# Two levels of Strassen for the weight products of layer 0 in a two-layer graph network kernel, with block sums lent to VectorE

## The chip, the cores and the metric

The kernel runs on one core of one Trainium2 chip. The metric is the device time in microseconds (us) of one execution. All runs told here that were timed in rounds were in the fast state. A profile is one execution taken by the hardware profiler; its span is about 2 us shorter than the time of the same run, and a little different from run to run.

## The reference

128 graphs of 128 nodes, 512 features, all fp32. Cut to what matters:

```python
# layer 0
deg = jnp.sum(adj, axis=-1, keepdims=True)
agg = jnp.einsum('bij,bjf->bif', adj, x) / jnp.maximum(deg, EPS)
out = jax.nn.relu(jnp.einsum('bnf,of->bno', concat([x, agg]), W))
x   = _layernorm(x + out)
# layer 1: three times adj @ (x @ W) + b, with relu after the first two
x   = _layernorm(x + gcn3(gcn2(gcn1(x))))
```

The kernel rewrites layer 0 as `x @ WA + adj_normalized @ (x @ WB)`. These two, `x @ WB` (called y) and `x @ WA`, are the "weight products of layer 0". The graphs go in 32 groups of four; a group's layer 1 is interleaved with the next group's layer 0.

## The kernel before

Everything is planned ahead by a list scheduler in the kernel's own Python. Each operation names its engine, an estimated length, what it reads and writes, and whether it uses the SBUF port that VectorE and GpSimd share. The planner keeps a clock per engine and one for the shared port, and returns an order, in which the operations are then emitted. It counts as users of the port every GpSimd operation and VectorE's sums with both inputs in SBUF; VectorE's sums that read PSUM, and its small layernorm instructions, it lets pass.

```python
class Plan:
    AHEAD = 24
    ...
    def start(o, t):
        ...
        if o.shared:
            port = (o.engine, end)
    ...
            for e in engines[1:]:
                ...
                can = [
                    o for o in known[e]
                    if ready_at[o] <= t and has_room(o, t) and not (o.shared and port[0] != e and port[1] > t)
                ]
                ...
                o = min(can, key=lambda o: (o.latest, o.n))
                ...
                start(o, t)
```

The emission is two lines. Note what they do not contain: the port is a clock in the planner and nothing else.

```python
    for o in plan.order():
        o.emit()
    return plan
```

A 512x512 weight product is one level of Strassen-Winograd: 7 block products of 4 matmuls with 256 columns. Sums of data blocks go to GpSimd, sums of weights to VectorE, PSUM partial results through ScalarE copies and VectorE sums.

```python
    class Data:
        def sums(self):
            for d, a, b, op in ((4, 2, 3, OP.add), (5, 4, 0, OP.subtract), ...):
                add("POOL", F, const(self.t[:, d]), const(self.t[:, a]), const(self.t[:, b]), ...)
    ...
    def product(p, a, b, k, start, transposed):
        ...
            for o in range(2):
                for c in range(2):
                    ...
                    nc.tensor.matmul(bank_ap(p)[:, o, :], lhsT, rhs, ...)   # 256 columns
    ...
    def wino_a(key, a, b, c00, c11, transposed=False, inner=None):
        product(py, a, b, 1, True, transposed)
        s1 = copied(py)                       # ScalarE, PSUM to SBUF
        product(pz, a, b, 5, True, transposed)
        ...
```

The last product of a group, which matters below, multiplies the adjacency by a 512-wide row block `row` that VectorE has to take out of PSUM first:

```python
    def seg_last(q, m):
        s, u = row(q, "s3"), u_of(q)
        ...
            nc.tensor.matmul(bank_ap(p)..., a[:, g, :], s.t[:, g, :], start=True, stop=True, ...)
        # then + u, layernorm, store
```

## Time and profile before

The median was 2423.59 us in the three runs known ahead of the prediction, and 2424.42 us (2420.16 to 2426.06, four runs) with one more.

| | before |
|---|---|
| span of the profile | 2426.3 us |
| TensorE busy | 2390.6 us, 99% |
| VectorE, ScalarE, GpSimd busy | 36%, 33%, 37% |
| TensorE work, matmuls times their spacing | 2382 us |
| one group in the steady part | 74.47 us |

The page's lines and how they are read stand in the prediction. In one sentence: TensorE runs at its own spacing from 80 us to the end, but for some 10 us, so its work is nearly the whole time, and the other engines have two thirds of theirs free.

### The profile page before, as it was taken

To read this page: it belongs to the slowest core of one execution; us is meant where nothing else is said; L and a number is where in the kernel's file an instruction comes from. 1 tells how busy PE (TensorE), PEld (TensorE's weight loads), DVE (VectorE), ACT (ScalarE), POOL (GpSimd) and SP (SyncE) were. 2 spreads that over 40 slices of the span, in tenths; PEclk is the share of its full clock that TensorE was granted. 3 is DMA by queue.
4 is the path that set the end of the run, shared out by engine and by line. 5 is a ranking of instruction groups with operands and counts; after the bars stand their busy time and mean duration, and the time that the engine had idled before them with its cause. 6 is when DMAs were issued, how large, how long until landed. Compare 5 with 4: busy or idle time off the path is not lost.

```text
span 2426.3 us, 29271 instructions
## 1 busy us (share of the span) xinstructions
PE 2390.6 (99%) x11776; PEld 2079.8 (86%) x11776; DVE 864.1 (36%) x1685; ACT 800.6 (33%) x1345; POOL 895.2 (37%) x772
## 2 busy tenths in 40 slices
PE   7999999999999999999999999999999999999997
PEld 6888888888888888888888888888888888888886
DVE  5433332333333333332343333333323433233323
ACT  2233333233332333233333333333233333333333
POOL 3333433334333344332443333433334432344323
PEclk9999999999999999999999999999999999999999
DMA  8201211112111121110111111211111111011100
GB/s 208 57 30 63 66 49 57 44 48 65 53 56 48 40 65 57 53 61 27 65 57 53 61 41 51 66 57 53 51 37 61 53 48 61 22 61 55 42 18 35
DMA packets 56360, 133.30 MB, mean 55 GB/s; under 512 B 21920, under 2 KB 27040, under 8 KB 48160
## 3 DMA queue, kind: packets, MB, share of 16 engines
q1 hardware_dynamic: 55552, 131.16, 16.9%
q8 instruction: 93, 1.52, 0.3%
q14 instruction: 43, 0.35, 0.1%
q10 hardware_dynamic: 672, 0.26, 0.1%
HBM read 97.78 MB, written 33.62 MB: 54 GB/s over the span
## 4 chain that ended last, share of the span: by engine, by line
PE 95%; DMA 3%; DVE 1%; issue 0%; ACT 0%; SPq 0%; POOL 0%; ACTq 0%; POOLq 0%; DVEq 0%
PE bank L408 77%; PE bank L646 5%; PE bank L687 5%; PE bank L421 4%; PE bank L563 4%; DMA dd<-deg 2%; DMA r<-dd 1%; DMA xT<-in_xT_dram 0%; DVE st L489 0%; SPq L265 0%; DVE deg L374 0%; DVE ah L275 0%; DVE row L275 0%; DVE deg L375 0%; ACT s L394 0%
## 5 line engine op out<-in xcount | busy, mean ns | idle before, releaser
L273 POOL TENSOR_TENSOR T<-T 128x512 f32<-128x512 f32 x384 | 484.9, 1274 | 1225.0 <-ACT T L656 970.1
L408 PE MATMUL bank<-w,T 128*128 128x256 f32 x3584 | 800.1, 379 | 2.3 <-ACT s L394 2.3
L408 PEld LDWEIGHTS bank<-w,T 128*128 128x128 f32 x3584 | 675.9, 190 | 92.8 <-ACT s L394 2.3
L394 ACT COPY s<-bank 128x512 f32<-128x512 f32 x480 | 281.3, 586 | 1225.5 <-PE bank L408 1225.2
L275 DVE TENSOR_TENSOR row<-bank,s 128x512 f32<-128x512 f32 x288 | 198.8, 691 | 690.5 <-PE bank L408 545.3
L408 PE MATMUL bank<-wb,xT 128*128 128x256 f32 x1792 | 404.5, 380 | 6.0 <-DMA wb<-in_w0T_dram 5.6
L408 PEld LDWEIGHTS bank<-T,w 128*128 128x128 f32 x1792 | 340.3, 190 | 74.5 <-issue 31.3
L408 PE MATMUL bank<-T,w 128*128 128x256 f32 x1792 | 397.8, 379 | 1.5 <-issue 1.5
L408 PE MATMUL bank<-wa,xT 128*128 128x256 f32 x1792 | 397.7, 379 | 0.0
L408 PEld LDWEIGHTS bank<-wb,xT 128*128 128x128 f32 x1792 | 341.5, 191 | 53.3 <-issue 5.6
L408 PEld LDWEIGHTS bank<-wa,xT 128*128 128x128 f32 x1792 | 340.5, 190 | 46.3
L273 POOL TENSOR_TENSOR u<-u,b 128x512 f32<-128x512 f32 x128 | 164.3, 1285 | 188.0 <-PE bank L563 186.4
L273 POOL TENSOR_TENSOR xT<-xT 128x512 f32<-128x512 f32 x128 | 163.8, 1280 | 61.6 <-DMA xT<-in_xT_dram 49.4
L563 PEld LDWEIGHTS bank<-at,u 128*128 128x128 f32 x1024 | 130.9, 195 | 12.4 <-ACT u L506 6.8
L563 PE MATMUL bank<-at,u 128*128 128x128 f32 x1024 | 132.3, 279 | 6.4 <-ACT u L506 6.4
L275 DVE TENSOR_TENSOR bank<-bank,s 128x512 f32<-128x512 f32 x96 | 67.2, 700 | 195.3 <-PE bank L421 195.3
L421 PE MATMUL bank<-row,ah 128*128 128x256 f32 x512 | 126.2, 379 | 2.3 <-DVE ah L275 2.3
L687 PE MATMUL bank<-row,at 128*128 128x512 f32 x256 | 120.5, 594 | 5.6 <-DVE row L275 5.6
L646 PEld LDWEIGHTS bank<-at,row 128*128 128x128 f32 x1024 | 119.4, 192 | 1.7
L530 DVE SCALAR_TENSOR_TENSOR u<-bank,x 128x512 f32<-128x512 f32 x128 | 88.3, 690 | 89.7 <-PE bank L421 87.5
L590 ACT ACTIVATE T<-T,b 128x256 f32<-128x256 f32 x192 | 90.5, 503 | 89.0 <-DVE T L275 89.0
L646 PE MATMUL bank<-at,row 128*128 128x128 f32 x1024 | 119.5, 275 | 0.0
(30 smaller groups left out, 1226.1 us busy)
## 6 DMA issues: line engine op xcount, KB each, us to landing
x<-in_x_dram SPq DMA_DIRECT2D x32, 1024.0 KB, 6.5
out_dram<-o SPq DMA_DIRECT2D x64, 512.0 KB, 2.6
xT<-in_xT_dram SPq DMA_DIRECT2D x31, 1024.0 KB, 4.8
ar<-in_adj_dram SPq DMA_DIRECT2D x32, 256.0 KB, 2.8
at<-in_adjT_dram SPq DMA_DIRECT2D x32, 256.0 KB, 2.6
r<-dd SPq DMA_DIRECT2D x31, 256.0 KB, 4.5
w<-in_w_dram SPq DMA_DIRECT2D x12, 256.0 KB, 10.1
xT<-in_xT_dram SPq DMA_DIRECT2D x4, 256.0 KB, 5.0
```

The lines of the kernel that those rows point to most:

```text
L273: gpsimd(n, lambda: pinned(nc.gpsimd.tensor_tensor(dst(), a(), b(), op=op)), reads, writes)
L275: vector(n, lambda: pinned(nc.vector.tensor_tensor(dst(), a(), b(), op=op)), reads, writes, shared)
L394: scalar(512, lambda: pinned(nc.scalar.copy(S_T[s.index], bank_ap(p))), [p], [s])
L408: nc.tensor.matmul(bank_ap(p)[:, o, :], lhsT, rhs, start=start and o == 0 and c == 0, stop=c == 1, skip_group_check=True,)
L421: nc.tensor.matmul(bank_ap(p)[:, j, :], AH_T[:, g, :], y.t[:, g, h * H : (h + 1) * H], start=False, stop=True, skip_group_check=True,)
L530: nc.vector.scalar_tensor_tensor(u.ap(m, h), bank_ap(p), 0.0, X.ap(m, h), op0=OP.max, op1=OP.add)
L563: nc.tensor.matmul(bank_ap(p)[:, c // 2, (c % 2) * P : (c % 2 + 1) * P], u.t[:, g, c * P : (c + 1) * P], a[:, g, :], start=True, stop=True ...
L590: lambda t=t, o=o: pinned(nc.scalar.activation(t, t, AF.Relu, bias=B1_T[:, 2 * h + o : 2 * h + o + 1])),
L646: nc.tensor.matmul(bank_ap(p)[:, g // 2, (g % 2) * P : (g % 2 + 1) * P], s.t[:, g, o * P : (o + 1) * P], a[:, g, :], start=True, stop=True ...
L687: nc.tensor.matmul(bank_ap(p).rearrange("p a n -> p (a n)"), a[:, g, :], s.t[:, g, :], start=True, stop=True, skip_group_check=True,)
```

## The change

It replaces the outer 7 products of layer 0's two weight products by 7 x 7 inner ones: 49 matmuls of 128 columns for 28 matmuls of 256 columns, which in 128-column units is 49 for 56. For this it needs block sums of block sums. Per group there are eight more sums of x, six sums that combine the inner results (and two that finish), and many PSUM evacuations with 384 elements. GpSimd alone could not take all these in time, so the planner may give a GpSimd block sum to VectorE when it is urgent (`HELP`). To fit, the diff also reorders the blocks of x, y and u, keeps fewer buffers for the adjacency, loads and sums the next group's adjacency later in the group, and stores each graph's output apart; no run separates these.

The diff, cut to its core (cuts marked `...`):

```diff
+    AHEAD, HELP = 24, 4.0
...
+                if e == "DVE":
+                    can += [
+                        o for o in known["POOL"]
+                        if o.other and ready_at[o] <= t and o.latest + slip < t + self.HELP and has_room(o, t)
+                        and not (port[0] != e and port[1] > t)
+                    ]
...
+                known[o.engine].remove(o)
+                if o.engine != e:
+                    o.engine, (o.us, o.emit) = e, o.other
...
+        def inner_sums(self):                      # class Data
+            for ps in BATCH:                       # 4 of the 7 outer blocks, then 3
+                t, ti = self.t[:, ps[0] : ps[-1] + 1], self.ti[:, :, ps[0] : ps[-1] + 1]
+                a00, a10, a01, a11 = (t[:, :, c, g] for c in range(2) for g in range(2))
...
+                    add("POOL", len(ps) * P, const(dst), const(a), const(b), reads, writes, op)
...
+    def inner_product(p, a, b, ps, i, start):
+        parts = [(a.inner(k, i), b.inner(k, i)) for k in ps]
+        def emit():
+            for n, ((ta, _), (tb, _)) in enumerate(parts):
+                    nc.tensor.matmul(quarters(p, 4)[:, n], ta, tb, ...)     # 128 columns
...
     def seg_y_a(q):
         y = row(q, "y")
-        wino_a(("y", q), XA, WB, sums_to(y, 0, 0), sums_to(y, 1, 1))
+        def c11(u3, p5, keys):
+            add("POOL", F, const(y.ap(1, 1)), u3, p5, keys, y.block(1, 1))
+        outer_a(("y", q), XA, WB, c11)
...
     XA.sums()
     WB.sums()
+    XA.inner_sums()
+    WB.inner_sums()
```

`XI_T` (written `xI` in the profile) holds the new inner sums of x; `xT` the blocks of x and their outer sums; `T` the blocks of layer 1's data; `v` the half-combined inner results.

## The prediction

> **What bounds the kernel now.** I read the page's first two parts, then the chain that ended last, then the instruction groups by shape, then a table of stretches and the timeline of the start.
>
> ```profile
> span 2426.3 us, 29271 instructions
> PE 2390.6 (99%) x11776; PEld 2079.8 (86%) x11776; DVE 864.1 (36%) x1685; ACT 800.6 (33%) x1345; POOL 895.2 (37%) x772
> PE 95%; DMA 3%; DVE 1%; issue 0%; ACT 0%; SPq 0%; POOL 0%; ACTq 0%; POOLq 0%; DVEq 0%
> ```
>
> TensorE is busy 99% and makes up 95% of the chain; the other three engines are idle for two thirds of the span. "Busy" is not yet "at its rate", so the spacing of matmuls has to come from the chain. One group of four graphs in the steady part:
>
> ```profile
> 1112.71 34.53 PE bank L408 x160
> 1148.11 3.57 PE bank L646 x32
> 1157.73 10.36 PE bank L408 x48
> 1173.33 1.78 PE bank L563 x16
> 1175.11 1.72 PE bank L687 x4
> ```
>
> Columns: start, length, what. There are two matmul records for each fp32 matmul of the program (11776 records for 5888). A 256-column record takes 34.53/160 = 0.2158 us, a 128-column one 1.78/16 = 0.1113 us (3.57/32 = 0.1116 in the other place), a 512-column one 1.72/4 = 0.43 us. The group rows' means (379 and 279 ns) are pipelined durations and not spacings: 160 records of 379 ns would not fit into 34.53 us.
>
> ```profile
> 0.00:51.48 51.48, 36.82 (x161) 31.80 (x161) 29.75 (x52) 9.87 (x15) 11.22 (x12) 0.90 0.90 229
> 437.76:1112.71 674.95, 670.73 (x3314) 584.09 (x3313) 236.13 (x469) 224.76 (x379) 250.62 (x216) 1.00 0.17 53
> 1112.71:2304.18 1191.47, 1191.47 (x5890) 1038.10 (x5889) 416.64 (x818) 399.97 (x673) 445.48 (x384) 1.00 0.16 52
> ```
>
> Columns: stretch, length, busy time of PE, PEld, DVE, ACT, POOL, then clock, DMA share, GB/s. In the last stretch, sixteen groups (74.47 us each), TensorE never stops. Counting the built program: 1024 matmuls of 128 columns, 4736 of 256, 128 of 512. At two records each: 1024 x 0.2226 + 4736 x 0.4316 + 128 x 0.86 = 228 + 2044 + 110 = 2382 us. The span is 2426, so 44 us are gaps: about 20 before the second layer's first product at 51.5 us, about 16 behind the last matmul and between the lone last group's steps, and some 8 in the middle, mostly a wait for the degrees' round trip through DRAM. The kernel is TensorE plus a start and an end.
>
> **What the Trainium skill says.** (1) "TensorE: Matmul & The Clock Gate", section "Back-to-back issue gap": a warm matmul costs N/2.4 + 2.5 ns, and in streams of weight load and matmul pairs both set the spacing. The trace fits if an fp32 record streams twice its columns: 512/2.4 + 2.5 = 215.8 ns for 256, and 109 for 128. (2) Same page, "LDWEIGHTS (loading the stationary operand)": P/1.2, so 107 ns for 128 columns whatever follows. A 128-column matmul is thus as short as a weight load can hide under; the measured 111.3 to 111.6 ns, with a fresh weight per matmul and waits every few matmuls, says that it is still hidden, at 2% over the formula. I use the measured number. (3) "SBUF — State Buffer", section "SBUF: two separate sides": VectorE with two SBUF inputs and GpSimd hold a shared port pair exclusively, and the loser waits out the whole instruction. The trace agrees: the same 512-element VectorE sum of weights takes 0.68 us alone and 1.2 us beside GpSimd:
>
> ```profile
> 7.00 4.92 DVE L275 TENSOR_TENSOR wb<-wb 128x512 f32<-128x512 f32 x4 [6.13 <-DMA wb<-in_w0T_dram]
> 8.43 5.85 POOL L273 TENSOR_TENSOR xT<-xT 128x512 f32<-128x512 f32 x4 [7.99 <-DMA xT<-in_xT_dram]
> 18.28 0.68 DVE L275 TENSOR_TENSOR wa<-wa 128x512 f32<-128x512 f32 x1
> ```
>
> (4) "GPSIMD Engine Reference", section "Engine selection": a two-input sum is about half as fast there as on VectorE. The rows agree:
>
> ```profile
> L273 POOL TENSOR_TENSOR T<-T 128x512 f32<-128x512 f32 x384 | 484.9, 1274 | 1225.0 <-ACT T L656 970.1 <-ACT T L618 232.9 <-ACT T L573 7.1
> L275 DVE TENSOR_TENSOR row<-bank,s 128x512 f32<-128x512 f32 x288 | 198.8, 691 | 690.5 <-PE bank L408 545.3 <-ACT s L394 144.0
> ```
>
> **The change, part by part.** *TensorE.* A layer-0 product was 7 block products of 4 matmuls of 256 columns, 28 x 0.4316 = 12.08 us. It becomes 49 matmuls of 128 columns, 49 x 0.2226 = 10.91 us: 1.18 us less, twice per group, so 2.35. It is not 49/56 of the time, because a half-length matmul costs 0.1113 and not 0.1079. The aggregation had 8 matmuls of 256 (3.45 us) and gets 2 of 256 and 12 of 128 (0.86 + 2.67 = 3.53): 0.08 more. Net 2.27 us per group, 32 groups: 72.7 us. The built program says the same: 4544 x 0.2226 + 2752 x 0.4316 + 110 = 2310 us, against 2382.
>
> *VectorE and GpSimd.* Per group there are now eight inner sums of x, six more sums in the outer combination, two finishing ones, and PSUM evacuations of 384 elements. Since the planner may give block sums to VectorE, the count in the built program matters: SBUF-only sums on VectorE go from 52 to 630 of 512 elements plus 103 of 384, PSUM ones gain 480 of 384; GpSimd falls from 640 to 454 (plus 33 short ones). At 0.69 us, an estimated 0.53 for 384 elements (three quarters of 0.691 and a little), and 1.28 on GpSimd: VectorE 864 + 399 + 55 + 254 = about 1570 us (67% of 2350), GpSimd 895 - 237 + 32 = 690 us (29%). ScalarE gains 32 copies of 0.59, 19 us. No engine comes near TensorE's 98%, so in the steady part these lie beside it. I also looked at each turn in which TensorE waits for another engine that itself waits for TensorE: in the order of the changed program, all but some 30 of about 1700 such waits have at least 0.75 us more TensorE work in between than one evacuation needs (0.59 us on ScalarE, 0.69 on VectorE, 0.15 for signals). In the kernel before 90 had only 0.25 to 0.5 us to spare, and they did not stall.
>
> *The start.* This is what the change adds to the path. Before, TensorE starts at 5.6 us on raw blocks. Now even the first inner product is accumulated over four blocks, three of them sums, so seven outer sums stand ahead of it on VectorE (spaced 0.60 us when alone: instructions start at 18.28, 18.88 and 19.48 us in the timeline): first matmul near 12 us. Then VectorE has a hundred instructions before the layernorm scale that releases the first graph product (before: some 40): about 52 of 512 elements at 0.60 us spacing, 32 of 384 at 0.47, a dozen small ones, 48 us, some 5 us of port collisions, and two or three of waits. From 7 us on that ends near 63, where the kernel before began its graph products at 44.9. TensorE has by then about 31 us of work in front of them (10.9 + 10.9 + 3.5 + 5.6 pulled in from the next group), so 32 us idle, against 20 before: +12 us. The three weight matrices of layer 1 and everything later wait no longer than before, and the end of the kernel is unchanged.
>
> *Sum.* 2423.6 - 72.7 + 12 = 2363. For drift between planned and real order in the steady part (port collisions, in-order VectorE) I add 3: **2366 us**, 2.4% less.
>
> **Rivals.** *VectorE becomes the bound in stretches.* It goes from 36 to 67% and is in order, with evacuations queued behind block sums and sums held out by GpSimd. For: it is the only engine whose load nearly doubles, and before there were three places where TensorE stopped because VectorE stood at a degree reduction waiting for a transfer. Against: the slack above. If each of 32 groups lost 1 us, 2395; that would be "within 2%". *The 128-column matmul does not hold its spacing* where two thirds of all records are such, each with another weight and a wait every 6 to 8. For: 107 ns of weight load in a slot of 111 ns has no room. Against: both places where the trace has such streams hold it, up to 32 in a row. 2 ns more would cost 7040 added records x 2 ns, 14 us: 2380. *The start costs nothing*, because GpSimd is free there and the degrees' transfers (11 us) already hold layer 0 up to 38 us before: then 2352. *Or it costs 25*, if the long VectorE list meets more collisions: 2378. *Transfers* become more and smaller (128 stores for 64, split loads of x); at 16% share they stay hidden.
>
> **Range and chances.** TensorE's gain is sure to about 8 us; the start may be 0 to 25 us worse; steady stalls 0 to 30, rather few. That gives 2345 to 2392. The limit for 2% is 2375.1. Faster by over 2%: 0.70; within 2%: 0.28; slower by over 2%: 0.02.
>
> **What would show it.** In the changed profile: a chain over 90% PE, with inner-product pieces at 0.111 us per record (wrong if 0.115 or more); a steady group of 72.2 us instead of 74.47; a stretch table in which PE stays at its length and VectorE at some two thirds; first graph product at 60 to 66 us; the idle of TensorE before it near 32 us. If the steady group is 73.5 us with TensorE waiting for VectorE, the first rival holds. If the VectorE sums of block data average well over 0.75 us, the port collides more than the plan allowed for.

## The result, and the profile after

The changed kernel is correct and takes 2453.41 us (median of 4 runs, 2452.49 to 2456.52); the kernel before took 2424.42 us in the same rounds. The ratio is 1.0125 (95% interval 1.0107 to 1.0142). Ratios here are the mean time of one kernel's fast runs over that of the other's of the same rounds, so not quite the ratio of the medians. So the change cost 1.2% where 2.4% were expected to be won, and the time is outside the predicted range of 2345 to 2392.

From the page of the changed kernel: span, busy time of the engines, and the chain that ended last by engine.

```profile
span 2450.7 us, 36879 instructions
PE 2344.8 (96%) x14848; PEld 2120.0 (87%) x14848; DVE 1666.5 (68%) x2878; ACT 817.3 (33%) x1377; POOL 777.8 (32%) x619
PE 82%; DVE 16%; issue 2%; DMA 0%; ACT 0%; POOL 0%; SPq 0%; ACTq 0%; DVEq 0%; POOLq 0%
```

TensorE's share of the chain has fallen from 95% to 82%, and VectorE has come in with 16%, although VectorE is busy only 68% of the span. An engine that is idle a third of the time sets the end here. The stretch table of the steady part agrees (columns as in the prediction):

```profile
1110.00:2300.00 1190.00, 1155.23 (x7353) 1045.39 (x7352) 815.82 (x1392) 404.25 (x683) 386.86 (x305) 1.00 0.16 52
```

TensorE is idle for 35 us of these 1190, where before it never stopped. What it waits for stands in one line of the waits (columns: who waited for what, us in total, how many times, longest):

```profile
PE bank L875 <- DVE row L288: 63.0, 29, 2.2
```

29 waits of 2.2 us, about one per group, all in front of the group's last product, all for VectorE's evacuation of `row`. The TensorE work itself is as planned: an inner product's pieces hold 0.111 us per record, as in this line of the timeline (start, length, what), 0.89 us from one piece of eight to the next:

```profile
1189.36 1.05 PE L518 MATMUL bank<-wb,xT 128*128 128x128 f32 x8
1190.25 1.06 PE L518 MATMUL bank<-wb,xI 128*128 128x128 f32 x8
1191.14 1.06 PE L518 MATMUL bank<-wb,xT 128*128 128x128 f32 x8
```

So why is `row` late? First the VectorE groups by shape (line, engine, operation, out<-in, shape, count, then busy time and mean length in ns of one, then idle before). Six sums into `xI` per group, and the sums of `T`:

```profile
L288 DVE TENSOR_TENSOR T<-T 128x512 f32<-128x512 f32 x216 | 201.0, 950 | 102.4 <-ACT T L810 60.2 <-ACT T L848 37.9 <-POOL T L290 2.2
L288 DVE TENSOR_TENSOR xI<-xI,xT 128x512 f32<-128x512 f32 x32 | 54.0, 1687 | 0.0
L288 DVE TENSOR_TENSOR xI<-xT 128x512 f32<-128x512 f32 x32 | 52.9, 1654 | 0.0
L288 DVE TENSOR_TENSOR xI<-xT 128x384 f32<-128x384 f32 x31 | 48.1, 1551 | 0.0
L288 DVE TENSOR_TENSOR xI<-xT,xI 128x512 f32<-128x512 f32 x32 | 21.7, 679 | 0.0
```

Three of the six sums into `xI` last 1.55 to 1.69 us in the mean of all groups, while one of the same shape takes 0.68 us. They do not sum slowly; they are held out. By whom, the timeline of one such place shows (VectorE's, GpSimd's and TensorE's rows; other rows cut):

```profile
1260.14 2.50 POOL L290 TENSOR_TENSOR xT<-xT 128x512 f32<-128x512 f32 x2 [3.90 <-PE bank L754]
...
1261.38 1.28 DVE L676 TENSOR_SCALAR rstd<-mv 128x2 f32<-128x2 f32 x1
...
1263.39 3.26 POOL L290 TENSOR_TENSOR u<-u,b 128x512 f32<-128x512 f32 x2
1263.77 3.29 DVE L288 TENSOR_TENSOR xI<-xT 128x512 f32<-128x512 f32 x2
...
1266.61 1.58 POOL L290 TENSOR_TENSOR xT<-xT 128x512 f32<-128x512 f32 x1
...
1266.99 2.22 DVE L288 TENSOR_TENSOR xI<-xI,xT 128x512 f32<-128x512 f32 x2
...
1269.13 1.15 DVE L288 TENSOR_TENSOR xI<-xT,xI 128x512 f32<-128x512 f32 x2
1270.20 0.68 DVE L288 TENSOR_TENSOR row<-bank,s 128x512 f32<-128x512 f32 x1
...
1270.94 1.98 PE L875 MATMUL bank<-row,at 128*128 128x512 f32 x4 [2.18 <-DVE row L288]
```

Read it downwards. From 1263.39 to 1268.2 GpSimd adds the bias b3 to `u` twice and makes a sum of `xT`; from 1263.77 on VectorE makes sums into `xI`. While both are at work each of VectorE's takes 1.65 us and each of GpSimd's 1.6: one waits out the other, turn by turn. As soon as GpSimd is through, two sums take 1.15 us together. `row` stands behind these six in VectorE's queue. It starts 6.43 us after the first of them, and TensorE has by then been idle for 2.18 us.

In the order that the planner returned, GpSimd's two additions and its `xT` sum come after VectorE's sums into `xI`. GpSimd ran them before. Nothing in the program tells it not to: their data are ready, it waits for no semaphore of VectorE's, and nothing else is left ahead of them in its own queue. In the built program, by my count, 204 of GpSimd's 487 sums are free to start before the VectorE block sum that stands ahead of them in the plan (a recount from the planner's dependencies alone gives some 250). The plan's turns on the port are not in the program.

To see where all the time went I took, in each trace, the distance from one TensorE record to the next, less the record's own spacing (0.1113, 0.2158 or 0.43 us by shape). Columns 1 and 2 are what the change did:

| us | before | after | GpSimd waits (below) | first group one level (below) |
|---|---|---|---|---|
| TensorE work | 2382.1 | 2309.4 | 2309.4 | 2311.7 |
| until the first matmul | 5.6 | 9.4 | 9.1 | 6.1 |
| lost from there to 80 us | 16.4 | 32.8 | 30.7 | 22.7 |
| lost from 80 us to the last matmul | 10.3 | 88.9 | 8.7 | 6.3 |
| behind the last matmul | 12 | 10 | 10 | 10 |
| span | 2426.3 | 2450.7 | 2368.1 | 2356.9 |

The 72.7 us of work are won. The start takes back 20, and the stretch behind it 79, of which 63.0 us are the 29 waits above; of the other 26 us that are lost there, some 16 are TensorE records next to these waits that come at a wider distance, and 9.5 lie elsewhere, about as much as in the kernel before.

### The profile page after: what moved, and what is told of

It is laid out like the page before. It is cut to its first block, busy times and chain, and to the rows that moved or that the text cites. A ratio compares the mean times of both kernels' runs of the same rounds, so it can differ in the third digit from the quotient of the medians.

```text
span 2450.7 us, 36879 instructions
## 1 busy us (share of the span) xinstructions
PE 2344.8 (96%) x14848; PEld 2120.0 (87%) x14848; DVE 1666.5 (68%) x2878; ACT 817.3 (33%) x1377; POOL 777.8 (32%) x619
## 4 chain that ended last, share of the span: by engine, by line
PE 82%; DVE 16%; issue 2%; DMA 0%; ACT 0%; POOL 0%; SPq 0%; ACTq 0%; DVEq 0%; POOLq 0%
PE bank L488 42%; PE bank L518 26%; DVE xI L288 7%; PE bank L838 5%; PE bank L531 4%; PE bank L875 3%; PE bank L754 3%; DVE row L288 2%; DVE xT L288 2%; DVE rstd L676 1%; PE bank L500 1%; DVE st L672 1%; DVE bank L288 1%; DVE u L727 1%; DMA xT<-in_xT_dram 0%
## 5 line engine op out<-in xcount | busy, mean ns | idle before, releaser
L488 PE MATMUL bank<-w,T 128*128 128x256 f32 x3584 | 821.3, 379 | 2.9 <-ACT s L474 2.9
L488 PEld LDWEIGHTS bank<-w,T 128*128 128x128 f32 x3584 | 659.3, 190 | 82.3 <-ACT s L474 3.2
L290 POOL TENSOR_TENSOR T<-T 128x512 f32<-128x512 f32 x168 | 213.6, 1279 | 884.3 <-DVE T L288 876.5
L488 PE MATMUL bank<-T,w 128*128 128x256 f32 x1792 | 403.7, 380 | 0.1
L488 PEld LDWEIGHTS bank<-T,w 128*128 128x128 f32 x1792 | 333.5, 190 | 52.8 <-issue 10.4
L288 DVE TENSOR_TENSOR v<-bank,s 128x512 f32<-128x512 f32 x192 | 132.2, 689 | 205.0 <-ACT s L474 113.7
L288 DVE TENSOR_TENSOR T<-T 128x512 f32<-128x512 f32 x216 | 201.0, 950 | 102.4 <-ACT T L810 60.2
L288 DVE TENSOR_TENSOR row<-bank,s 128x512 f32<-128x512 f32 (+1 forms) x288 | 179.9, 642 | 120.2 <-PE bank L488 102.1
L290 POOL TENSOR_TENSOR xT<-xT 128x512 f32<-128x512 f32 (+1 forms) x126 | 172.9, 1383 | 138.2 <-PE bank L754 112.7
L288 DVE TENSOR_TENSOR s<-bank,v 128x384 f32<-128x384 f32 x192 | 107.0, 558 | 150.6 <-PE bank L518 146.2
L288 DVE TENSOR_TENSOR v<-v 128x512 f32<-128x512 f32 x189 | 149.3, 790 | 9.9 <-DVE v L288 0.5
L518 PEld LDWEIGHTS bank<-wb,xT 128*128 128x128 f32 x896 | 115.7, 196 | 31.1 <-issue 23.2
L754 PEld LDWEIGHTS bank<-at,u 128*128 128x128 f32 x1024 | 124.7, 192 | 19.2 <-issue 15.6
L518 PE MATMUL bank<-wb,xT 128*128 128x128 f32 x896 | 124.7, 280 | 16.7 <-DMA xT<-in_xT_dram 9.4
L518 PEld LDWEIGHTS bank<-wb_i,xT 128*128 128x128 f32 x896 | 120.8, 193 | 10.6 <-DVE wb_i L288 1.4
L754 PE MATMUL bank<-at,u 128*128 128x128 f32 x1024 | 124.7, 275 | 1.3 <-ACT u L689 1.3
```

The lines of the kernel that those rows point to most:

```text
L288: on_vector = lambda: pinned(nc.vector.tensor_tensor(dst(), a(), b(), op=op))
L290: on_gpsimd = lambda: pinned(nc.gpsimd.tensor_tensor(dst(), a(), b(), op=op))
L488: nc.tensor.matmul(bank_ap(p)[:, o, :], lhsT, rhs, start=start and o == 0 and c == 0, stop=c == 1, skip_group_check=True,)
L518: nc.tensor.matmul(quarters(p, 4)[:, n], ta, tb, start=start and n == 0, stop=True, skip_group_check=True)
L754: nc.tensor.matmul(bank_ap(p)[:, c // 2, (c % 2) * P : (c % 2 + 1) * P], u.chunk(g, c), a[:, g, :], start=True, stop=True, skip_group_chec ...
```

## The experiments

Two theories are tested. **Theory A**: the plan's port turns are not enforced, GpSimd goes ahead of its turn, VectorE's in-order queue is late, and TensorE waits. **Theory B**, the rival: VectorE simply has too much to do around the last product, whoever has the port (the first rival of the prediction).

### 1. The plan's port order, enforced

The order of instructions stays as it is. Wherever an operation that uses the port follows one of the other engine in the plan, it now waits for it.

```diff
+    port = None
     for o in plan.order():
-        o.emit()
+        ins = o.emit()
+        if o.shared and ins is not None:
+            if port is not None and port[0] != o.engine:
+                tc.add_manual_dep(ins.ins, port[1].ins.name, <semaphore wait>, reason="port")
+            port = o.engine, ins
```

> The changed kernel with the same instructions in the same order on every engine, plus semaphore waits that make VectorE and GpSimd take the shared SBUF port in the order in which the planner gave it to them (in the changed kernel 204 of GpSimd's 487 sums are free to start before the VectorE block sum that stands ahead of them). Theory A (the gap of 2.2 us per group before the last product is VectorE's block sums being held out by GpSimd sums that start early): the sums of xT into xI fall from 1.55 to 1.75 us to 0.55 to 0.7, TensorE's wait for the row evacuation falls from 63 us to under 15, time 2380 (2365 to 2400). Theory B (VectorE has too many instructions ahead of the evacuation, port or not): the wait stays above 45 us, time 2440 to 2456. Theory C (the order holds, but holding GpSimd back makes its own sums late): a new wait of TensorE for GpSimd sums, time 2400 to 2440.

Measured: correct, 2376.22 us (2374.84 to 2377.03, 4 runs), the kernel before at 2430.55 (7 runs), ratio 0.9777 (0.9759 to 0.9795). Its page, and VectorE's groups by shape:

```profile
PE 2330.1 (98%) x14848; PEld 2121.5 (89%) x14848; DVE 1553.4 (65%) x2878; ACT 814.6 (34%) x1377; POOL 688.4 (29%) x619
PE 98%; DVE 1%; issue 0%; POOL 0%; ACT 0%; DMA 0%; SPq 0%; ACTq 0%; DVEq 0%; POOLq 0%
```

```profile
L288 DVE TENSOR_TENSOR T<-T 128x512 f32<-128x512 f32 x216 | 143.7, 685 | 101.9 <-ACT T L810 60.2 <-ACT T L848 37.9 <-POOL T L290 1.9
L288 DVE TENSOR_TENSOR xI<-xT 128x512 f32<-128x512 f32 x32 | 21.7, 679 | 0.0
L288 DVE TENSOR_TENSOR xI<-xI,xT 128x512 f32<-128x512 f32 x32 | 21.7, 679 | 0.0
```

TensorE's row for the last product, which in the changed kernel had 63.0 us of idle time before it:

```profile
L875 PE MATMUL bank<-row,at 128*128 128x512 f32 x256 | 120.4, 593 | 0.0
```

Not one instruction was moved, removed or made smaller; waits were only added, and the kernel became 3.4% faster than the changed kernel in ratio to the kernel before (0.9777 against 1.0125). The wait before the last product is gone. The group is now 72.28 us in the mean (26 groups from the fourth on), against 75.12 in the changed kernel and 74.71 before (counted the same way, so with the degree waits in it; a group without one took 74.47). VectorE's and GpSimd's busy times fall by 113 and 89 us: that was the time spent held out, counted as busy. Theory B falls: VectorE does the same work in the same order.

### 2. Only one of the two waits

Which of the two engines goes ahead of its turn to harm? Two kernels, each with one half of the waits.

```diff
-            if port is not None and port[0] != o.engine:
+            if port is not None and port[0] != o.engine and o.engine == "POOL":   # GpSimd waits
+            if port is not None and port[0] != o.engine and o.engine == "DVE":    # VectorE waits
```

> The changed kernel with the same order of instructions, and waits between neighbours on the shared SBUF port only where GpSimd is the one that follows (GpSimd waits for VectorE's sums that stand ahead of it; VectorE waits for nothing new). Theory A (GpSimd starts its sums some 4 us before its turn, and the in-order VectorE delivers row late): this half is the one that matters, so the time is 2370 to 2385 us, sums into xI average 0.6 to 0.75 us, and the idle time before L875 is gone. Rival (both directions matter, VectorE running into GpSimd's turn costs as much): 2400 to 2430 us.

> The other half: VectorE waits for GpSimd's sums that stand ahead of it, GpSimd waits for nothing new. Theory A: the early GpSimd sums stay, so sums into xI stay at 1.5 to 1.75 us, the gap of about 2.2 us before L875 stays, and the time is 2445 to 2465 us. Rival (any wait that separates the two cures it): 2375 to 2400 us.

Measured, on one chip, with the kernel before at 2427.89 us (7 runs): GpSimd waits, 2372.59 us (2369.88 to 2377.81, 4 runs), ratio 0.9775 (0.9753 to 0.9796). VectorE waits, 2497.4 us (2495.12 to 2498.33, 4 runs), ratio 1.0285 (1.0266 to 1.0304). Both are correct. The half that makes GpSimd wait does all that the whole does. The other half is worse than no wait at all, and by more than I expected (the range ended at 2465). The wait before the last product is what it was in the changed kernel, 63.0 us, and a second one has come: layer 1's products (L488) now wait 24.8 us for sums into `T`, where the changed kernel shows 0.1 us of idle in this row. Two rows of the page's groups, and the changed kernel's row for layer 1's products:

```profile
L488 PE MATMUL bank<-T,w 128*128 128x256 f32 x1792 | 403.9, 380 | 24.8 <-DVE T L288 23.6
...
L875 PE MATMUL bank<-row,at 128*128 128x512 f32 x256 | 135.9, 657 | 63.0 <-DVE row L288 63.0
```

```profile
L488 PE MATMUL bank<-T,w 128*128 128x256 f32 x1792 | 403.7, 380 | 0.1
```

That fits a VectorE which now also stands still for GpSimd, while GpSimd still goes ahead of its turn; which of its waits made up these 25 us I did not separate. They are not all of the loss against the changed kernel: the trace also has 14 stretches at half the granted clock between 80 and 2400 us, 47.8 us in all, where the changed kernel has 3 with 10.2, so TensorE runs slowly for a part of the time.

The same place in the kernel where GpSimd waits (its timeline, other rows cut), to be laid beside the one of the changed kernel:

```profile
1221.76 1.15 DVE L288 TENSOR_TENSOR xI<-xT 128x512 f32<-128x512 f32 x2
...
1222.17 1.88 PE L875 MATMUL bank<-row,at 128*128 128x512 f32 x4
...
1222.83 1.15 DVE L288 TENSOR_TENSOR xI<-xI,xT 128x512 f32<-128x512 f32 x2
...
1223.90 1.15 DVE L288 TENSOR_TENSOR xI<-xT,xI 128x512 f32<-128x512 f32 x2
...
1224.97 0.68 DVE L288 TENSOR_TENSOR row<-bank,s 128x512 f32<-128x512 f32 x1
...
1225.13 0.69 POOL L677 TENSOR_TENSOR rstd<-rstd,neg_half 128x2 f32<-128x2 f32 x1 [4.51 <-DVE xI L288]
...
1225.78 2.50 POOL L290 TENSOR_TENSOR u<-u,b 128x512 f32<-128x512 f32 x2
...
1226.57 1.88 PE L875 MATMUL bank<-row,at 128*128 128x512 f32 x4
```

The six sums take 3.21 us to the start of `row` (6.43 there). GpSimd waits 4.51 us, as the bracket says, and does its additions afterwards in 1.25 us each. TensorE's row has no bracket: no wait. GpSimd has 71% of the span free, so its wait costs nothing.

### 3. The additions that go ahead, left out

A check of Theory A from the other side, without new waits: the same order, but the bias additions `u<-u,b` on GpSimd are planned and not emitted. (b3 is zero in these inputs, so the result stays right.)

```diff
             add("POOL", F, const(u.graph(g)), const(u.graph(g)), const(b), ...)
+            plan.ops[-1].skip = True
...
     for o in plan.order():
-        o.emit()
+        if not getattr(o, "skip", False):
+            o.emit()
```

> The changed kernel with the same order on every engine, but the additions of the last bias to u (four per group, 128 in all, nearly all on GpSimd) are not emitted; the bias is zero in this input, so the result should still agree. VectorE's list is the same but for two instructions. Two of the GpSimd sums that run beside the xI sums are these. Theory A: the xI sums lose most of their holding out, the gap before the last product shrinks from 2.2 us to under 0.7 us in a group, time 2385 to 2410. Theory B: VectorE's list is as long as before, so the gap stays, 2440 to 2456.

Measured: correct, 2380.82 us (2380.44 to 2382.96), ratio 0.9799 (0.9778 to 0.9821), somewhat faster than expected (2385 to 2410). The two sums that the additions used to hold out are at full speed again; a third is still held out by the `xT` sum that remained on GpSimd. These are VectorE's groups by shape:

```profile
L288 DVE TENSOR_TENSOR xI<-xI,xT 128x512 f32<-128x512 f32 x32 | 54.9, 1715 | 0.0
L288 DVE TENSOR_TENSOR xI<-xT 128x512 f32<-128x512 f32 x32 | 21.7, 678 | 0.0
```

TensorE's row for the last product (line 876 in this kernel) has 0.7 us of idle time left in all groups together:

```profile
L876 PE MATMUL bank<-row,at 128*128 128x512 f32 x256 | 123.2, 604 | 0.7
```

So the delay is a sum of turns: with GpSimd's three turns in a row TensorE waits 2.2 us, with one left the room suffices, but only just.

### 4. No lending: all block sums on GpSimd

```diff
-    AHEAD, HELP = 24, 4.0
+    AHEAD, HELP = 24, -1e9
```

> The changed kernel without the freedom to give block sums to VectorE: all of them on GpSimd, the order planned anew. VectorE falls from 68% to about 47%, GpSimd rises from 32% to about 62%. Theory A: no VectorE sum competes for the port in the steady part, its sums stay at 0.69 us, but the chain of 12 sums at 1.28 us for the next x on GpSimd stands before the next first product, so that TensorE waits for GpSimd instead: 2440 to 2500. Theory B (VectorE's load is what hurts): taking a third of its load away gives 2360 to 2400.

Measured: 2505.42 us (2503.56 to 2508.78), ratio 1.0311 (1.029 to 1.0332), and a wrong result (relative error 0.133), which was not on purpose. GpSimd's busy share is 60%, and TensorE waits in front of layer 1's products and of the inner products instead of the last product. So without the lending, in the order that was then planned, the kernel is slower still. Because of the wrong result I looked further, with two single runs (so their state is unknown), of which the first enforces the port order as in experiment 1, and the second puts the inner sums of x on VectorE and nothing else:

> The kernel with all block sums on GpSimd gave a wrong result (relative error 0.133) for a reason unknown. The same with port waits in both directions: if two engines met on data at a moment that the waits now exclude, the result is right; if the fault lies in the order of instructions or in GpSimd's own work on these shapes, it is wrong again by the same 0.133. Time 2480 to 2560 us either way, as GpSimd's 46 us a group stay and now wait as well.

> As the kernel with all block sums on GpSimd, but the sums into xI (and the in-place inner sum of xT) go to VectorE, the others to GpSimd. If GpSimd's work on those shapes made the result wrong, it is right here; if not, wrong again. GpSimd has 8 sums less per group (about 9 us), so 2440 to 2490 us.

Measured: with waits 2507.68 us, wrong by the very same relative error (0.1333790); with the inner sums of x on VectorE 2456.76 us and correct. So it is not a matter of timing. Whether GpSimd computes one of these shapes differently, or this other order of instructions has a fault, these runs leave open. The simulator that checks a program before it goes to the chip decides it; this was looked up when the document was checked. There the output of this experiment's program differs from the changed kernel's by 0.13338 as well, the one with the inner sums of x on VectorE agrees exactly with the changed kernel, and the wrong one stays wrong by exactly as much when VectorE does all its block sums in the same order. So the fault is in the order of the instructions, and not in how GpSimd adds; which instruction stands in the wrong place was not looked for. The changed kernel and the fast versions do nearly all these sums on VectorE (the exceptions: the in-place sum of 384 elements, and one single sum into `xI`) and are correct. As the time of a wrong result, 2505 is weak evidence for the lending. The correct 2456.76, in which only the inner sums of x are on VectorE, is 1.009 times the kernel before of the same rounds (2434.81), so no slower than the changed kernel (1.0125), though slower than the versions with lending and port waits; it was a single run without the port waits. That the lending as such is not what costs the time is shown by experiment 1, which keeps it and stands at 0.9777.

### 5. The control: the waits on the kernel before

The same waits as in experiment 1, on the kernel before.

```diff
 # in the kernel before
     for o in plan.order():
-        o.emit()
+        # the loop of experiment 1
```

> A control: the kernel before, with 56 products, and the same port waits in both directions as in the first experiment. Theory A (the 2.3 us per group come from 49 products, and the waits only keep them from being lost again): there is no time for the waits to win here, since TensorE stands idle only some 8 us between 80 and 2400 us of this kernel, so 2418 to 2434 us, ratio 0.996 to 1.003. Rival (the waits alone are what made the first experiment fast): 2370 to 2400 us.

Measured: correct, 2438.66 us (19 runs) against 2434.81 (22 runs) in the same rounds, ratio 1.0012 (0.9998 to 1.0027). The time lies a little above the range that was expected, but on this chip the kernel before does too; the ratio is inside the expected 0.996 to 1.003. The waits win nothing there. The gain of experiment 1 is the 49 products; the waits only keep it.

### 6. The start: the first group by one level

The remaining difference to the prediction is the start. Theory A for it: the first group's inner products stand behind block sums, which for all other groups are made long before. This kernel has all waits of experiment 1, does the first group's layer 0 with the old 56 products, and makes the inner sums of the weights after it.

```diff
-    XA.inner_sums()
-    WB.inner_sums()
...
-            seg_y_a(t)
+            seg_y_a(t) if t else one_y_a(t)       # one level, as in the kernel before
...
+        if t == 0:
+            WB.inner_sums()
+            WA.inner_sums()
```

> The kernel with all port waits, and group 0's layer 0 by one level as in the kernel before (56 products), the other 31 groups by two levels; the inner sums of the weights come after group 0's layer 0. Theory A (the start lost its 20 us to the block sums that group 0's 49 products wait for): first graph product back at 45 to 52 us, about 16 us won at the start, 2.3 us more TensorE work in group 0, so 2356 to 2366 us. Rival (the start is held by the transfers and the degree reciprocal whatever layer 0 is): 2372 to 2380 us.

Measured: correct, 2358.06 us (2357.3 to 2358.94, 4 runs), ratio 0.9712 (0.9691 to 0.9732). It ran on the same chip and in the same rounds as the kernels of experiment 2, so it is 14.5 us faster than the one in which GpSimd waits. That one has half of the waits and this one has them all; the kernel of experiment 1, which has them all and does the first group by two levels, stood at 0.9777. This version beats both kernels. TensorE's start in the two, the changed kernel first:

```profile
9.37 0.77 PE L518 MATMUL bank<-wb,xT 128*128 128x128 f32 x2 [9.37 <-DMA xT<-in_xT_dram]
...
28.29 0.94 PE L518 MATMUL bank<-wb_i,xI 128*128 128x128 f32 x6 [2.94 <-DVE s L288]
...
49.41 1.10 PE L500 MATMUL bank<-row,ah 128*128 128x256 f32 x4 [3.88 <-DVE ah L288]
...
64.24 3.36 PE L518 MATMUL bank<-wb,xT 128*128 128x128 f32 x14 [6.60 <-POOL xT L290]
...
72.89 2.94 PE L754 MATMUL bank<-at,u 128*128 128x128 f32 x24 [1.31 <-ACT u L689]
```

```profile
6.06 3.75 PE L488 MATMUL bank<-wb,xT 128*128 128x256 f32 x8 [6.06 <-DMA wb<-in_w0T_dram]
...
42.06 5.29 PE L500 MATMUL bank<-row,ah 128*128 128x256 f32 x16 [6.95 <-DVE ah L288]
...
54.90 5.75 PE L809 MATMUL bank<-at,u 128*128 128x128 f32 x32 [2.39 <-ACT u L689]
```

The first graph product (L754, here L809) comes at 54.9 and not 72.9, later than the 45 to 52 I expected and than the 44.9 of the kernel before. In the table above the start's loss is 28.8 us (6.1 + 22.7) against 42.2 in the changed kernel and 22.0 before: two thirds of what the start cost (against 45.2 with all waits, in experiment 1, somewhat more). What is left, some 7 us, I can only point at: the wait of 6.95 us for `ah`, the normalized adjacency, which was 2.26 us in the kernel before. No run separates it.

## Why the prediction was wrong

**The TensorE step was right.** 72.7 us less work was predicted, and 72.7 come out of the count of records at the predicted spacings. These are the measured ones: the 128-column spacing held at 0.111 us per record (second rival: falls). With the port order enforced the group is 72.28 us long, where 72.2 was predicted (from 74.47).

**The failed step is the "3 us" of drift in the steady part.** It rested on the sentence that "all but some 30 of about 1700 such waits have at least 0.75 us more TensorE work in between than one evacuation needs". That count looked one hop back: one evacuation against the TensorE work beside it. But the evacuation stands in an in-order queue, and what counts is everything ahead of it there. In the fast version the bank that `row` is taken from is complete at 1222.3 and `row` is needed at 1226.6: more than 4 us of room, which passed the count easily. 3.21 us of it are sums into `xI` that stand ahead of `row`, and if each of three waits for a turn of GpSimd's, that becomes 6.4 and the room is overdrawn by 2.2. I had cited the lock and its number, but had taken the plan's turns on the port as if they were executed. They were worth 79 us, not 3.

**The rival was named, sized too small, and its reason was another.** "VectorE becomes the bound in stretches" was sized at 1 us a group; it was about 2.5. And it is not VectorE's load (65% in the fast version, and no wait), it is GpSimd's early start. The prediction's own test caught it: sums of block data on VectorE "well over 0.75 us" would mean more collisions than planned, and they were 0.95 us for `T` and 1.55 to 1.69 for half of those into `xI`.

**The start was mis-sized.** +12 us predicted, +20.2 measured (42.2 for 22.0). The first matmul came earlier than predicted (9.4, not near 12), the first graph product later (72.9, not 60 to 66). The idle time was about right: 9.4 us and 23.2 us of gaps, near the 32 of the prediction. What was missing is that TensorE also runs part of the first 80 us at a lower granted clock: 0.89 in the mean, against 0.94 before. That and slow first records cost 9.5 us against 4.6; no run separates the two. The comparison was uneven, too: the prediction's 32 us is idle time alone, while its 20 for the kernel before is all that TensorE lost up to 51.5 us, slow records included. In one measure the idle time is 32.6 us for 17.4. Experiment 6 shows that most of the start's loss hangs on the first group's inner products.

**VectorE and GpSimd** were predicted at 1570 and 690 us; the changed kernel shows 1666.5 and 777.8, and with the order enforced 1553.4 and 688.4. So the counting of instructions was right, and the difference was time held out at the port.

With the port order enforced the rest of the sum holds: the version in which GpSimd waits loses 17.8 us at the start (39.8 for 22.0) in place of 12, and takes 2372.59 us, 7 more than the 2366 predicted, in rounds in which the kernel before took 2427.89 and not 2423.6.

## What to carry to other kernels

A planner that takes turns on a shared resource plans nothing unless the program enforces the turns: where two in-order engines share a port, put a semaphore wait on the engine that has time to spare, here GpSimd, so that it cannot go ahead (here the wait on the other engine made it worse). When you ask whether an evacuation is in time, count all that stands ahead of it in its engine's queue at the length it has under collisions, not the one instruction. And an engine can set the end at 68% busy, so look for single waits that return once per group rather than at busy shares.

## What the Trainium skill lacked or had wrong

- "SBUF — State Buffer", section "SBUF: two separate sides", is right that the port pair is held for a whole instruction, but does not say how two queues that both have sums ready share it. Here two engines that both had sums ready took turns: a 512-element sum on VectorE took 1.65 to 1.69 us for 0.68 alone, one on GpSimd about 1.6 for 1.27, and even a VectorE instruction on 128x2 elements (L676 in the timeline of the changed kernel) took 1.28 us beside GpSimd, where the same line took 0.17 us at 1255.29. What no page says: a semaphore wait on the GpSimd side brought the 512-element sums into `xI` and `T` back to 0.68 to 0.69 us and won more than it cost, ratio 0.9775 for 1.0125.
- "TensorE: Matmul & The Clock Gate", section "Part 1: The HAM clock gate (the "warmup" mystery)", gives, in its table of the two states, about 3.4 us of idle before the clock halves. Here 3 of the 29 waits of 2.2 us were followed by matmuls at half the clock, with only those 2.2 us of idle before them; the stretch table of the changed kernel shows the granted clock at 0.50 behind one of them:

```profile
1194.38 3.60 PE L875 MATMUL bank<-row,at 128*128 128x512 f32 x4 [2.18 <-DVE row L288]
```

```profile
1194.40:1196.00 1.60, 1.60 (x2) 0.81 (x3) 1.19 (x2) 1.52 (x2) 0.00 (x0) 0.50 0.00 0
```

  That page has no rate for fp32 matmuls either (another page counts passes through the array for them, without a time). In all kernels here one fp32 matmul is two records, of 0.2158 us each for 256 columns and 0.1113 us each for 128.
